# Routed rows scattered to token order, and two shared-expert tiles placed between the last two down products

## The chip, the cores and the metric

The kernel runs on 1 core of one Trainium2 chip. The metric is device time in microseconds for one execution; the median of 3 runs before the change is 1626.27 us (1625.15 to 1630.43). The profile is of one further execution.

## The reference

One layer over 1250 tokens of width 768, in float32: a graph network and a linear attention added to the tokens, and then a mixture-of-experts feed-forward, which is the part that matters here.

```
x = x + gnn(layernorm(x)) + linear_attention(layernorm(x))
xn = layernorm(x)
probs = softmax(xn @ router_w)                  # 8 experts
gates, idx = top_k(probs, 2); gates /= sum(gates)
routed = sum over the 2 picks: gate * ((silu(xn @ w_gate[e]) * (xn @ w_up[e])) @ w_down[e])
shared = (silu(xn @ ws_gate) * (xn @ ws_up)) @ ws_down      # hidden width 384
alpha  = sigmoid(xn @ sg_w + sg_b)
out = x + alpha * shared + (1 - alpha) * routed
```

Each expert has three 768x768 matrices (2304 KB each).

## The kernel before, in words

Tokens are kept as 10 tiles of 125 (`TP`, `NT`). `acc` holds the running sum of the layer on chip. After the graph and attention parts, each tile is normalised, written to DRAM as `xd` (by row) and transposed into `xnT`.

**Routing.** Each token has two picks, r = 0 and 1: 2500 rows of work. They are sorted by expert into parts of 64 rows (`PART`); two parts make a block of 128 rows. There are at most 26 blocks (`NBLK`), of which 22 (`NSURE`) always run; the others stand in nested `tc.If`s on the count of parts. `slot[:, r, t]` is the place of a row in that order. The DRAM table `who` takes, for each slot, the number of its token: 20 scatters on POOL's DMA queue (L898). It is then read back as `ids` (L904), on SP's queue.

**Shared expert.** While the tables are made, PE computes the shared expert's hidden rows into `hTs_s` (L942); its down product is left for the end of the kernel.

**Blocks.** For each block, `gather` fetches 128 rows of `xd` by index (POOL's queue, L973). `fetch(j, 0)`, `(j, 1)`, `(j, 2)` load the block's gate, up and down matrices into two-buffer rings `wg`, `wu`, `wd` (SP's queue, L985; the expert's number is read by a register load, L983). `rows` transposes the gathered rows, `gate` and `up` make the hidden rows, `hidden` transposes those, `down` makes the block's output. `product` (L1002) takes each half of the block from one of the two buffers of a ring, so that a block can straddle two experts; a fetch for the next block therefore waits for the present block's product with the same ring. The loop is software-pipelined by hand: in round j stand gate(j), hidden(j-1), up(j), rows(j+1), down(j-1). After each `down`, DVE copies the result out of PSUM (L1032) and ACT's queue writes the 128 rows to `ys` (L1033), block by block. `rings`' third member `wd` is allocated where `xnT` and the shared expert's weights lay; the other two are allocated earlier. Fetches are issued for one block beyond the 22.

**Join.** After the nested `tc.If`s (L1067) each engine meets the untaken path, on which its semaphores are stepped as the blocks would have done; before that, an engine that owns a DMA queue waits for its own transfers in flight.

**Combination.** For each token tile two gathers (POOL's queue, L1089) fetch the two rows of each token from `ys` by `slot`; PE makes the shared down product (12 matmuls of 125x384, L1097), and DVE adds `alpha` times it (L1100) and the two gated rows (L1102) to `acc`. Then the tile is stored, 120 rows by SP's queue and 5 by ACT's (L1105, L1106). `g2` holds the gates times 1 - `alpha`, `al` holds `alpha`.

The order on each engine is made by a tile framework from the program order and from the buffers: a scheduler can move an instruction ahead of others that it doesn't depend on, and waits are semaphores on engines and DMA lanes.

Of the kernel before, what the change touches and what calls it, by code (L numbers as in the profile page):

```python
# [8 lines left out]
F32 = mybir.dt.float32  # L9
# [53 lines left out]
def gps_block(ctx: ExitStack, tc: tile.TileContext, x, src, dst, norm_g, norm_b, W1, a_src1, a_dst1, b1,  # L63
# [7 lines left out]

    xd = dram.tile([N, D], F32, name="xd")
    who = dram.tile([NSLOT, 1], I32, name="who")
    ys = dram.tile([NSLOT, D], F32, name="ys")
    xd_t = xd.rearrange("(t p) d -> t p d", p=TP)
    who_b = who.rearrange("(b p) o -> b (p o)", p=P)
    who_p = who.rearrange("(b p) o -> p (b o)", p=P)
    ys_b = ys.rearrange("(b p) d -> b p d", p=P)
# [243 lines left out]
    with tc.tile_pool(name="cnt", bufs=1, reuse_waits="tile") as cp, \  # L322
# [3 lines left out]
        zero = cp.tile([P, D], F32, name="zero")  # L326
        nc.gpsimd.memset(zero, 0.0)
        nc.sync.dma_start(who_b, zero[:NBLK, :P].bitcast(I32))
        for j in range(NSURE, NBLK):
            nc.sync.dma_start(ys_b[j], zero)  # L330
# [282 lines left out]
    with tc.tile_pool(name="h2p", bufs=1, reuse_waits="tile") as hp, tc.tile_pool(name="gatw", bufs=2, reuse_waits="tile") as pw:  # L613
# [29 lines left out]
        ids = fp.tile([P, NBLK], I32, name="ids")  # L643
# [168 lines left out]
    with tc.tile_pool(name="fln", bufs=2, reuse_waits="tile") as pw, tc.tile_pool(name="flnps", bufs=2, space=PSUM, reuse_waits="tile") as ps:  # L812
# [17 lines left out]
        number = pw.tile([TP, NT], I32, name="number", bufs=1)  # L830
        nc.gpsimd.iota(number, pattern=[[TP, NT]], base=0, channel_multiplier=1)
# [64 lines left out]
        for t in range(NT):  # L896
            for r in range(2):
                put = nc.gpsimd.indirect_dma_start(  # L898
                    out=who, out_offset=bass.IndirectOffsetOnAxis(ap=slot[:, r, t:t + 1], axis=0),
                    in_=number[:, t:t + 1], in_offset=None, bounds_check=NSLOT - 1, oob_is_err=False)  # L900
                for p in puts:
                    tc.declare_no_dep(put.ins, p.ins, reason="slots differ")
                puts.append(put)
# [50 lines left out]
    with tc.tile_pool(name="fps", bufs=1, space=PSUM, reuse_waits="tile") as ps:  # L954
# [16 lines left out]
        def gather(j):  # L971
            if j < NBLK:
                nc.gpsimd.indirect_dma_start(  # L973
                    out=xin[j % 2], out_offset=None, in_=xd,
                    in_offset=bass.IndirectOffsetOnAxis(ap=ids[:, j:j + 1], axis=0),
                    bounds_check=N - 1, oob_is_err=False)

        def fetch(j, i):

            if j >= NBLK:  # L980
                return
            if i == 0:
                experts[j] = nc.sync.value_load(blk[0:1, j:j + 1], min_val=0, max_val=NE - 1)  # L983
            w = (w_gate, w_up, w_down)[i]
            nc.sync.dma_start(rings[i][:, j % 2], w[bass.ds(experts[j], 1)].rearrange("o (k p) f -> p (o k) f", p=P))  # L985
# [42 lines left out]
        def down(j):  # L1028
            y = yo[j % 2]
            for s in two:  # L1030
                product(j, 2, pd[:, s], hTs[j % 2], s)
            nc.vector.tensor_copy(y.rearrange("p (s d) -> p s d", s=2), pd[:, :, :HALF])  # L1032
            nc.scalar.dma_start(ys_b[j], y)  # L1033


        for j in two:
            gather(j)
            for i in range(2):
                fetch(j, i)
            if j == 0:  # L1040
                fetch(j, 2)
        places(0)
        rows(0)
        for j in range(NSURE):
            gate(j, 0)
# [3 lines left out]
            if j > 0 and j + 1 < NSURE + 1:  # L1049
                fetch(j + 1, 0)  # L1050
            if j + 1 < NSURE:
                places(j + 1)
            for s in two:
                up(j, s)
            if j > 0 and j + 1 < NSURE + 1:
                fetch(j + 1, 1)
            gather(j + 2) if j + 2 < NSURE + 1 else None
            if j + 1 < NSURE:
                rows(j + 1)
# [3 lines left out]
        hidden(NSURE - 1)  # L1063
        down(NSURE - 1)
        fetch(NSURE, 2)

        with ExitStack() as deeper:  # L1067
            for j in range(NSURE, NBLK):
                deeper.enter_context(tc.If(n_part > j * NPART))
                gather(j + 1)  # L1070
# [4 lines left out]
                fetch(j + 1, 0)  # L1075
                for s in two:
                    up(j, s)
                fetch(j + 1, 1)
                hidden(j)
                down(j)  # L1080
                fetch(j + 1, 2)
# [3 lines left out]
    with tc.tile_pool(name="comb", bufs=1, reuse_waits="tile") as cb, tc.tile_pool(name="cps", bufs=3, space=PSUM, reuse_waits="tile") as ps:  # L1085
        ygs = [cb.tile([TP, D], F32, name=f"yg{i}") for i in range(2 * NT)]
        for t in range(NT):
            for r in range(2):
                nc.gpsimd.indirect_dma_start(  # L1089
                    out=ygs[2 * t + r], out_offset=None, in_=ys,  # L1090
                    in_offset=bass.IndirectOffsetOnAxis(ap=slot[:, r, t:t + 1], axis=0),
                    bounds_check=NSLOT - 1, oob_is_err=False)
        for t in range(NT):
            pd = ps.tile([TP, 2, 512], F32, name="pds")
            for s in range(2):
                for f in range(nh):
                    nc.tensor.matmul(pd[:, s, :HALF], hTs_s[:, f, t * TP:(t + 1) * TP],  # L1097
                                     wsd[:, f, s * HALF:(s + 1) * HALF], start=(f == 0), stop=(f == nh - 1))
            av = acc[:, t, :].rearrange("p (s d) -> p s d", s=2)
            nc.vector.scalar_tensor_tensor(av, pd[:, :, :HALF], al[:, t:t + 1], av, op0=ALU.mult, op1=ALU.add)  # L1100
            for r in range(2):
                nc.vector.scalar_tensor_tensor(acc[:, t, :], ygs[2 * t + r], g2[:, t, r:r + 1], acc[:, t, :],  # L1102
                                               op0=ALU.mult, op1=ALU.add)

            nc.sync.dma_start(out_t[:TP - 5, t, :], acc[:TP - 5, t, :])  # L1105
            nc.scalar.dma_start(out_t[TP - 5:, t, :], acc[TP - 5:, t, :])  # L1106

# [26 lines left out]
```

## Time and profile before

| what | value |
|---|---|
| median of 3 runs | 1626.27 us (1625.15 to 1630.43) |
| the profiled execution: time, span | 1627.49 us, 1625.8 us |
| mean granted TensorE clock | 0.977 |
| busy PE, DVE, ACT, POOL | 94%, 44%, 23%, 9% of the span |
| a block in the steady run, on PE | 25.13 us |
| PE idle before the down product, waiting for `wd` | 9.2 us, once |
| POOL gathers of `yg` | 20, 1.33 us each |
| DVE sums of `yg` rows, 125x768 | 20, 1.02 us each |
| PE shared down product | 120 matmuls, 42.0 us |

The page divides the span into busy shares by engine, names the chain of work that ended last, and lists groups of equal instructions with the idle time before them and what ended it. A line such as "PE A <- DMA B: 9.2, 1, 9.2" means that PE's instructions A waited for the transfer B for 9.2 us in total, once, at most 9.2 us. PE, DVE, ACT and POOL are the compute engines, SP only issues transfers; a "q" after a name is the engine's sequencer, which also issues its DMAs.

### The profile page before, as it was taken

To read this page: it belongs to the slowest core of one execution; us is meant where nothing else is said; L and a number is where in the kernel's file an instruction comes from. 1 tells how busy PE (TensorE), PEld (TensorE's weight loads), DVE (VectorE), ACT (ScalarE), POOL (GpSimd) and SP (SyncE) were. 2 spreads that over 40 slices of the span, in tenths; PEclk is the share of its full clock that TensorE was granted. 3 is DMA by queue.
4 is the path that set the end of the run, shared out by engine and by line. 5 is a ranking of instruction groups with operands and counts; after the bars stand their busy time and mean duration, and the time that the engine had idled before them with its cause. 6 is when DMAs were issued, how large, how long until landed. Compare 5 with 4: busy or idle time off the path is not lost. (4 is left out here: it accounts for less than half of the span.)

```text
span 1625.8 us, 18650 instructions
## 1 busy us (share of the span) xinstructions
PE 1528.3 (94%) x7123; PEld 855.5 (53%) x7123; DVE 720.8 (44%) x1329; ACT 368.0 (23%) x630; POOL 140.4 (9%) x174
## 2 busy tenths in 40 slices
PE   6899889998999989999899998999999999999966
PEld 5566544444455678995455553444444444444433
DVE  7889639411625468996598531111111111111106
ACT  3222211111101058870367300101001111011000
POOL 2211000000000000000000142000000000000014
PEclk9999989999999999999999999999999999999988
DMA  8100042001201110002111366788888888888858
GB/s 237 39 1 1 2 128 66 4 0 38 72 20 49 30 45 32 32 17 75 32 60 48 106 92 159 293 310 315 325 315 310 306 314 314 316 319 311 308 171 262
DMA packets 104756, 238.83 MB, mean 147 GB/s; under 512 B 15735, under 2 KB 38391, under 8 KB 104663
## 3 DMA queue, kind: packets, MB, share of 16 engines
q1 hardware_dynamic: 84749, 192.43, 35.1%
q0 software_dynamic: 14544, 35.83, 7.4%
q10 hardware_dynamic: 5370, 9.30, 1.6%
q8 instruction: 63, 1.03, 0.3%
q14 instruction: 30, 0.25, 0.1%
HBM read 219.45 MB, written 18.02 MB: 146 GB/s over the span
## 5 line engine op out<-in xcount | busy, mean ns | idle before, releaser
L1002 PE MATMUL pdb<-wd,hT 128*64 128x384 f32 (+1 forms) x1056 | 176.9, 492 | 9.2 <-DMA wd<-in_L_ffn_w_down_dram 9.2
L1002 PE MATMUL pgb<-wg,xT 128*64 128x384 f32 (+1 forms) x1056 | 179.9, 491 | 0.2 <-ACT xT L1009 0.2
L1002 PE MATMUL pub<-wu,xT 128*64 128x384 f32 (+1 forms) x1056 | 174.0, 486 | 0.0
L539 PE MATMUL pp<-wkv,xnT 128*125 128x512 f32 x360 | 162.0, 599 | 0.1
L621 PE MATMUL pa<-G,u 125*125 125x199 f32 x800 | 140.4, 336 | 11.1 <-DVE h L629 6.0
L621 PEld LDWEIGHTS pa<-G,u 125*125 125x125 f32 x800 | 135.6, 189 | 16.2 <-issue 7.2
L1002 PEld LDWEIGHTS pdb<-wd,hT 128*64 128x64 f32 x1056 | 74.8, 138 | 100.7 <-issue 97.5
L1002 PEld LDWEIGHTS pub<-wu,xT 128*64 128x64 f32 x1056 | 75.6, 137 | 94.6 <-issue 94.6
L1002 PEld LDWEIGHTS pgb<-wg,xT 128*64 128x64 f32 x1056 | 74.0, 138 | 91.4 <-issue 90.6
L539 PEld LDWEIGHTS pp<-wkv,xnT 128*125 128x125 f32 x360 | 66.0, 190 | 74.0 <-issue 73.6
L1032 DVE COPY y<-pdb 128x768 f32<-128x768 f32 x22 | 21.1, 957 | 188.9 <-PE pdb L1002 188.9
L418 PE MATMUL ph<-wg,xnT 128*125 128x400 f32 x240 | 102.1, 532 | 2.7 <-PEq L432 2.6
L1021 DVE TENSOR_TENSOR h<-h,pgb 128x384 f32<-128x384 f32 x44 | 24.4, 554 | 181.0 <-ACT h L1020 181.0
L601 ACT ACTIVATE eb<-r,g_ss 125x625 f32<-125x625 f32 x120 | 95.0, 816 | 22.9 <-DVE ea L602 22.9
L602 DVE TENSOR_TENSOR ea<-ea,eb 125x625 f32<-125x625 f32 x120 | 94.0, 804 | 13.6 <-ACT eb L601 8.1
L604 DVE SCALAR_TENSOR_TENSOR u<-ea,cntT 125x625 f32<-125x625 f32 x120 | 94.0, 804 | 12.5 <-PE pa L621 8.0
L486 DVE CUSTOM_DVE_ANT_0 junk<-ssb,absent 125x1250 bf16<-125x1250 f32 x60 | 87.7, 1462 | 13.8 <-DMA ssb<-g_srow_d 12.5
L1020 ACT ACTIVATE h<-pgb 128x384 f32<-128x384 f32 x44 | 21.6, 490 | 308.2 <-PE pgb L1002 308.2
L569 PE MATMUL pq<-xnT,wq 128*128 128x500 f32 (+1 forms) x216 | 81.5, 521 | 4.5 <-DMA wq<-in_L_mix_w_qkv_dram 3.7
L721 PE MATMUL pu<-wu,xnT 128*125 128x384 f32 x240 | 82.5, 489 | 2.0 <-DVE acc L726 2.0
L1026 DVE TENSOR_TENSOR h<-h,pub 128x384 f32<-128x384 f32 x44 | 24.4, 554 | 134.4 <-PE pub L1002 134.4
L582 PE MATMUL pu<-wp,at 128*125 128x384 f32 x240 | 80.4, 488 | 1.1 <-DVE acc L585 1.1
(247 smaller groups left out, 1699.2 us busy)
## 6 DMA issues: line engine op xcount, KB each, us to landing
wg<-in_L_ffn_w_gate_dram SPq DMA_DIRECT2D x23, 2304.0 KB
wu<-in_L_ffn_w_up_dram SPq DMA_DIRECT2D x23, 2304.0 KB, 10.2
wd<-in_L_ffn_w_down_dram SPq DMA_DIRECT2D x23, 2304.0 KB
ys<-y ACTq DMA_DIRECT2D x22, 384.0 KB, 7.1
r<-g_rrow_d POOLq DMA_DIRECT2D x12, 610.4 KB, 8.3
wq<-in_L_mix_w_qkv_dram SPq DMA_DIRECT2D x18, 384.0 KB, 3.4
wkv<-in_L_mix_w_qkv_dram SPq DMA_DIRECT2D x6, 768.0 KB, 4.6
acc<-in_x_dram POOLq DMA_DIRECT2D x10, 375.0 KB, 10.8
```

Source lines behind the costliest of these rows:

```text
L418: nc.tensor.matmul(ph[:, :2 * CG], xnT[:, k, tok], wg[:, k, s * 2 * CG:(s + 1) * 2 * CG], start=(k == 0), stop=(k == KD - 1))
L486: nc.vector.tensor_tensor_reduce(out=junk, in0=self.ssb, in1=absent[:, dt, :], scale=1.0, scalar=-3.0e38, op0=ALU.add, op1=ALU.max, accum_ ...
L539: nc.tensor.matmul(pp, xnT[:, k, tok], wkv[:, k, :, :], start=(k == 0), stop=(k == KD - 1))
L569: nc.tensor.matmul(pq[:, :qw], wq[:, k, :], xnT[:, k, tok], start=(k == 0), stop=(k == KD - 1))
L582: nc.tensor.matmul(pu[:, s, :HALF], at[:, k, i * TP:(i + 1) * TP], wp[:, k, s * HALF:(s + 1) * HALF], start=(k == 0), stop=(k == KD - 1))
L601: nc.scalar.activation(eb, r[:, 1, :], AF.Exp, bias=ss02[:, st, h:h + 1])
L602: nc.vector.tensor_max(ea, ea, eb)
L604: nc.vector.scalar_tensor_tensor(u, ea, 1.0, cntT[:, st, half * W:(half + 1) * W], op0=ALU.min, op1=ALU.mult)
L621: nc.tensor.matmul(pa[i][:, :CO + 1], u[:, i * TP:(i + 1) * TP], G[:, st, h, :CO + 1], start=(st == 0), stop=(st == NT - 1))
L721: nc.tensor.matmul(pu[:, :HALF], xnT[:, k, t * TP:(t + 1) * TP], wus[s][:, k, :], start=(k == 0), stop=(k == KD - 1))
L1002: nc.tensor.matmul(pt[part, :HALF], rows[:, k, part], w[:, k, s * HALF:(s + 1) * HALF], start=(k == 0), stop=(k == KD - 1))
L1021: nc.vector.tensor_mul(h, h, pgs[s][:, :HALF])
```

## The change

- `who` has two columns: the token (where a row is read) and the token plus r times 1250 (where its result goes). `number` holds both, for r = 0 and 1. Slots with no row get 0 and 2500.
- `ys` is no longer in slot order but in token order: 1250 rows for r = 0, 1250 for r = 1, and three rows at the end that are set to zero. `down` writes by an indirect scatter on POOL's queue, by `ids[:, j, 1]`; an index of 2500 is out of bounds and writes nothing. The zero writes of the blocks that may not run are gone.
- The combination loads both rows of a token tile with one ordinary load on SP's queue, 128 rows of which 125 are used: 10 loads instead of 20 gathers.
- The shared down product is a function, in two halves of 384. Two of its ten tiles stand between `hidden(NSURE - 1)` and `down(NSURE - 1)`, in the PSUM banks of the gate and up products; the other eight stay in the combination. There the sums of `yg` rows start after the fourth tile, two token tiles a step, and stores follow when both parts are in.
- Fetches and gathers are no longer issued for block 23 of the loop (j = 22); a block in a `tc.If` fetches its own. At the start `fetch(0, 2)` comes after the fetches of blocks 0 and 1.

```diff
-    who = dram.tile([NSLOT, 1], I32, name="who")
-    ys = dram.tile([NSLOT, D], F32, name="ys")
+    who = dram.tile([NSLOT, 2], I32, name="who")
+    ys = dram.tile([2 * N + P - TP, D], F32, name="ys")
...
-        zero = cp.tile([P, D], F32, name="zero")
-        nc.gpsimd.memset(zero, 0.0)
-        nc.sync.dma_start(who_b, zero[:NBLK, :P].bitcast(I32))
-        for j in range(NSURE, NBLK):
-            nc.sync.dma_start(ys_b[j], zero)
+        nobody = cp.tile([NBLK, P, 2], I32, name="nobody")
+        nc.gpsimd.iota(nobody, pattern=[[0, P], [2 * N, 2]], base=0, channel_multiplier=0)
+        nc.sync.dma_start(who_b, nobody.rearrange("b p o -> b (p o)"))
+        rest = cp.tile([P - TP, D], F32, name="rest")
+        nc.gpsimd.memset(rest, 0.0)
+        nc.sync.dma_start(ys[2 * N:, :], rest)
...
-        number = pw.tile([TP, NT], I32, name="number", bufs=1)
-        nc.gpsimd.iota(number, pattern=[[TP, NT]], base=0, channel_multiplier=1)
+        number = pw.tile([TP, 2, NT, 2], I32, name="number", bufs=1)
+        for r in range(2):
+            nc.gpsimd.iota(number[:, r], pattern=[[TP, NT], [r * N, 2]], base=0, channel_multiplier=1)
...
-            nc.scalar.dma_start(ys_b[j], y)
+            nc.gpsimd.indirect_dma_start(
+                out=ys, out_offset=bass.IndirectOffsetOnAxis(ap=ids[:, j, 1:2], axis=0),
+                in_=y, in_offset=None, bounds_check=2 * N - 1, oob_is_err=False)
+
+        def shared(t, banks):
+            for s, pt in enumerate(banks):
+                half = slice(s * HALF, (s + 1) * HALF)
+                for f in range(nh):
+                    nc.tensor.matmul(pt[:TP, :HALF], hTs_s[:, f, t * TP:(t + 1) * TP], wsd[:, f, half],
+                                     start=(f == 0), stop=(f == nh - 1))
+                nc.vector.scalar_tensor_tensor(acc[:, t, half], pt[:TP, :HALF], al[:, t:t + 1], acc[:, t, half],
+                                               op0=ALU.mult, op1=ALU.add)
...
         for j in two:
             gather(j)
             for i in range(2):
                 fetch(j, i)
-            if j == 0:
-                fetch(j, 2)
+        fetch(0, 2)
...
         for j in range(NSURE):
+            more = j + 1 < NSURE
...
-            if j > 0 and j + 1 < NSURE + 1:
+            if j > 0 and more:
                 fetch(j + 1, 0)
...
-            gather(j + 2) if j + 2 < NSURE + 1 else None
+            if j + 2 < NSURE:
+                gather(j + 2)
...
         hidden(NSURE - 1)
+
+        shared(0, pgs)
+        shared(1, pus)
         down(NSURE - 1)
-        fetch(NSURE, 2)
...
-        ygs = [cb.tile([TP, D], F32, name=f"yg{i}") for i in range(2 * NT)]
+        ygs = [cb.tile([P, 2, D], F32, name=f"yg{t}") for t in range(NT)]
         for t in range(NT):
-            for r in range(2):
-                nc.gpsimd.indirect_dma_start(
-                    out=ygs[2 * t + r], out_offset=None, in_=ys,
-                    in_offset=bass.IndirectOffsetOnAxis(ap=slot[:, r, t:t + 1], axis=0),
-                    bounds_check=NSLOT - 1, oob_is_err=False)
-        for t in range(NT):
-            pd = ps.tile([TP, 2, 512], F32, name="pds")
...
+            nc.sync.dma_start(ygs[t], bass.AP(tensor=ys.tensor, offset=ys.offset + t * TP * D,
+                                              ap=[[D, P], [N * D, 2], [1, D]]))
+
+        def store(t):
             nc.sync.dma_start(out_t[:TP - 5, t, :], acc[:TP - 5, t, :])
             nc.scalar.dma_start(out_t[TP - 5:, t, :], acc[TP - 5:, t, :])
+
+        done = []
+        for t in range(2, NT):
+            pd = ps.tile([TP, 2, 512], F32, name="pds")
+            shared(t, [pd[:, s, :] for s in range(2)])
+            if t == NT - 1:
+                store(t)
+            if t < 3:
+                continue
+            for u in range(2 * (t - 3), min(2 * (t - 3) + 2, NT)):
+                for r in range(2):
+                    nc.vector.scalar_tensor_tensor(acc[:, u, :], ygs[u][:TP, r, :], g2[:, u, r:r + 1], acc[:, u, :],
+                                                   op0=ALU.mult, op1=ALU.add)
+                if u < NT - 1:
+                    done.append(u)
+            while done and done[0] <= t:
+                store(done.pop(0))
```

## The prediction

> **What bounds the kernel now.** I read three stretches: where the expert blocks begin, their steady run, and the tail. The page names the tail as the chain that ended last, so it comes first.
>
> ```profile
> span 1625.8 us, 18650 instructions
> ...
> DMA 1%; issue 1%; POOL 0%; DVE 0%; POOLq 0%; DVEq 0%
> ```
>
> The chain's first piece stands at 1576.37 us: the 20 gathers of `yg` on POOL, their transfers, the sums on DVE. The timeline dates the end: last DVE sum over at 1621.81, span over at 1625.8, so 4.0 us for the last store. The waits of that stretch:
>
> ```profile
> POOL yg L1089 <- SPq L1067: 87.4, 1, 87.4
> ...
> PE pdb L1002 <- DMA wd<-in_L_ffn_w_down_dram: 9.2, 1, 9.2
> ...
> PE pds L1097 <- DVE acc L1100: 4.4, 1, 4.4
> ...
> PE pds L1097 <- ACTq L1067: 2.3, 1, 2.3
> ```
>
> PE stands 9.2 us before the last block's down product: `fetch(21, 2)` is issued as down(20) ends, and the next work is the product that needs it. SP's own waits hold a 9.2 us piece at L1067, the join of the untaken branch, where it waits for the weight load it had just issued for a block that never runs. The tail in time:
>
> ```profile
> 1555.97 9.79 PE L1002 MATMUL pdb<-wd,hT 128*64 x48 [9.22 <-DMA wd<-in_L_ffn_w_down_dram]
> ...
> 1565.77 0.37 SPq L985 DMA_DIRECT2D wd<-in_L_ffn_w_down_dram  x1
> 1565.82 0.96 DVE L1032 COPY y<-pdb 128x768 f32<-128x768 f32 x1 [18.85 <-PE pdb L1002]
> 1566.81 0.33 ACTq L1033 DMA_DIRECT2D ys<-y  x1
> ...
> 1577.39 1.28 POOL L1089 DMA_INDIRECT yg<-ys,slot  x1 [87.37 <-SPq L1067]
> ```
>
> From the copy's end (1566.78) to the first gather 10.6 us pass. The last of the 20 gathers is issued at 1608.58, 31.2 us after the first, 1.64 us apart, and the DMA engines are full beside them (stretches: busy columns PE, PEld, DVE, ACT, POOL, then PE clock, DMA share, GB/s):
>
> ```profile
> 1550.00:1558.00 8.00, 2.03 (x8) 0.95 (x10) 0.00 (x0) 0.00 (x0) 0.00 (x0) 0.50 0.62 240
> ...
> 1600.00:1605.00 5.00, 5.00 (x17) 2.88 (x16) 2.92 (x4) 0.00 (x0) 4.09 (x4) 1.00 1.00 313
> ...
> 1010.00:1015.00 5.00, 5.00 (x34) 2.23 (x32) 1.11 (x2) 0.49 (x1) 0.00 (x0) 1.00 1.03 413
> ...
> 1085.00:1110.00 25.00, 25.00 (x158) 11.39 (x156) 3.17 (x5) 2.70 (x6) 1.00 (x1) 1.00 0.87 314
> ```
>
> The last line is the steady run: PE busy all 25 us of a 25.13 us block, DMA at 0.87. PE bounds it. At its start PE waits for the first gather:
>
> ```profile
> 990.33 0.37 SPq L904 DMA_DIRECT2D ids<-who  x1
> ...
> 995.54 1.07 POOL L973 DMA_INDIRECT xin<-xd,ids  x1 [11.28 <-DMA ids<-who]
> ...
> 999.64 1.51 PE L1008 MATMUL ptr<-ident,xin 128*128 128x128 f32 x6 [7.68 <-DMA xin<-xd,ids]
> ```
>
> **The change part by part.** Times are of the profiled execution.
>
> *Setup.* A 26x256 iota and a 3-row memset stand for the 0.74 us memset on POOL; SP loses four 384 KB zero writes (33.2 to 36.9 us). SP's next load waits until 52.85 and the DMA engines stand at 0.00 in 40 to 50 us, so 0. If that cover were gone: 1.57 MB at the 389 GB/s of that stretch (245 at share 0.63), 4 us, a gain. The second iota of `number` (20 values a row; POOL idles 23.5 us before the `who` scatters) costs 0. The scatters and `ids` carry 8 bytes where they carried 4, with as many pieces: 0, bounded by plus 1 us.
>
> *Start of the blocks.* In the built order SP issues `fetch(0,2)` after the loads for block 1. Before, wd(0) stood behind 21 register loads of `blk` (0.61 us each, 12.8 us: 990.7 to 1003.4), and wg(1), wu(1) behind it. Now those two, 4.7 MB, go right behind `ids`, at about 991.4, and take until about 1005 at 413 GB/s. `gather(0)` at 995.5 falls among them. Alone it landed in 4.0 us; at share 1.03 the gather of 1018.96 took 6.2, and the median of all is 7.0. PE waits for it alone, so plus 2.2 to 3.0; I take **+2.8**, near the median (`ids` ahead of them may also end later: bound plus 5; a gain is excluded, as nothing before the gather got shorter). wd(0) leaves at about 1004, as before, and nothing waited for wg(1).
>
> *Steady run.* Each block's 384 KB leave by POOL's queue, not ACT's. Bytes are the same; rows of empty slots are out of bounds (22 x 128 - 2500 = 316 rows fewer). POOL has 1.00 us of 25 busy; the issue adds about 1. The scatter waits for DVE's `y` copy, and behind it stands the gather two blocks ahead: that moves from about 1061.8 to 1071.5, needed at 1110.9, cover 39 us against 8.6 us of landing at worst. Its scatter waits also for the one before, 25 us older. Here the skill speaks against the change: the DMA: Bandwidth & Descriptors page, "Issuing engine by pattern", gives plain loads and stores to the sync and scalar queues and calls that path generally faster. The rows: `ys` from ACT landed in a median 7.1 us, gathers from POOL in 7.0; alone, the 360 KB store took 3.0 and the gather 4.0. By the rule one would charge 1 us a block, 22 in sum, if anyone waited; `y` has two buffers, 25 us of cover, so only the last block's is exposed. I take **0** (bounds -0.5 and +2).
>
> *Last block.* 24 matmuls of two shared tiles now stand between hidden(21), over at 1546.7, and down(21). 48 such matmuls took 15.75 us, so 7.9, to 1554.6: inside the wait, which ends at 1555.9 as before. wu(22), now gone, landed 8.1 us after 1538.23, before wd(21) started, so I give no gain for it; at best wd lands 1.3 us earlier. DVE's four 125x384 sums (about 0.55 us each) end before the `y` copy. What is gained is the clock: 0.50 after the wait, so down(21) took 9.79 us against 7.96 elsewhere. It ends at 1563.85 instead of 1565.76: **-1.9** (bounds -3.2 and -0.5).
>
> *Join.* Copy over at 1564.9. Scatter from POOL, landing 4.3 us alone (nearest row, the two gathers at 996): 1569.2. POOL's join waits for all its transfers, then steps their semaphores (that one instruction took 1.08 us at 1489), which SP's first load waits for: 1570.4. First gather before: 1577.39. Of these 7.0 us, 1.9 are counted: **-5.1** (bounds -6.5 and -1; several such steps or a slow receipt would eat it). SP's 9.2 us wait goes with its load. PE's 2.3 us wait for ACT goes too, off the path.
>
> *Tail.* Twenty gathers become ten SP loads of 786 KB (128 rows, two runs of 3 KB). First landing: a 360 KB store alone took 3.0, so about 2.1 fixed, plus 786 KB at 370 GB/s (314 at share 0.86), 2.1, plus issue 0.4: 4.6 us, at 1575.0. Later ones every 2.1 us. DVE takes longer: two sums of 1.02 a tile and sixteen half sums of 0.55; after that landing 20 x 1.02 + 15 x 0.55 = 28.7 us, so **DVE becomes the bound**, ending at 1603.7. PE needs 96 x 0.328 = 31.5 us from 1564.6 and has three PSUM buffers: its fourth tile waits for DVE from 1576.4 to about 1578.8, then follows DVE. The skill's TensorE: Matmul & The Clock Gate page, "What's actually happening", puts the drop to half clock after about 3.4 us of idling; here a 4.4 us wait was followed by 0.62 and 0.63. At 2.4 us the rule says full clock, sum unchanged. If it dropped for one such window PE would lose 1.7 us, shared with DVE's slack: 0 to +1.5. Loads end at about 1594; 3.8 MB of stores follow behind them in SP's queue, about 11 us at 350 GB/s, so they drain with DVE. From first transfer's issue to last sum: 33.3 us instead of 44.4, **-11.1**. Last store 4.0 us, as before.
>
> Sum: +2.8 - 1.9 - 5.1 - 11.1 = **-15.3**; span 1610.5, with the 1.7 us around it (1627.49 against 1625.8) 1612.2. The profiled execution lies 1.2 above the median of 1626.27, so the median becomes **1611.0**.
>
> **The rivals.**
>
> *The tail is DMA-bound at its old rate.* 11.7 MB at 290 to 313 GB/s, seen with share 1.0, is 39 us: 1571 + 39 + 2 = 1612, not 1607.7, so 5 us worse: 1616. For it: reads and stores mix, and the stores use 120 rows. Against: those rates held gathers through POOL's queue, which the page's table puts at 298 GB/s of engine time (35.83 MB in 7.4% of the span), the loads' queue at 337.
>
> *Cheap start, quick join.* xin lands in 5, down(21) starts early: 1607.
>
> *Slower: the weights come late.* Each fetch has 17 us (wd issued at 1069.43, needed at 1086.5) and lands in 8 to 10.3. Scatter and gather now come back to back, just as wd is fetched: 0.39 MB more, 1.3 us. From a landing of 17.1 us each microsecond costs 21; at 18.2, 25 us, and 1636; the sign turns at 17.7. That is 6 us more than I see (10.3 + 1.3).
>
> *The tiles don't lie in the wait.* PE's built order puts them there; excluded.
>
> **How the numbers follow.** Main case 0.62 (1607 to 1615), DMA-bound tail 0.20 (1613 to 1620), cheap start 0.10 (1604 to 1608), a DMA-bound tail with start and join near their bad bounds (+2.2 and +4.1 more: 1622) 0.04, late weights 0.04. The range 1604.5 to 1619 leaves out the last two and the outer ends. 0.3% is 4.9 us, about what a measurement of this kernel tells from no change. Faster 0.93, same 0.03, slower 0.04.
>
> **What would show it.** PE's 9.2 us wait for wd gone or under 2 us; down(21) near 8 us; first `yg` load near 1573 (1570 plus the start's 2.8); DVE nearly solid from there, 29 us; PE's wait for the first xin 10 to 11 us; PE solid in the blocks with a period of 25.1. It is wrong if DVE waits for `yg` over 5 us in sum after the first, if PE waits for weights inside the blocks, or if the first load leaves after 1577.

## The result, and the profile after

| | median | runs | ratio to the kernel before, 95% interval |
|---|---|---|---|
| before | 1628.33 us | 1625.15 to 1630.43 | |
| after | 1605.24 us | 1604.45 to 1606.43 | 0.986 (0.9839 to 0.9882) |

The 1628.33 us are the median of four runs of the kernel before: the three named at the head and one more, taken beside the kernel after. The change is faster by 1.4%, some 23 us. The prediction said 1611.0 and a range from 1604.5 to 1619.0, so the time lies in the range, at its fast end. The profiled execution has a span of 1603.0 us, 22.8 us less than before (1625.8).

I cut both spans at the same seven events and compare stage by stage. The timeline dates each event: by the start of a line, and for the copy of `y` and the last sum by the end of the line (start plus duration).

| stage | before | after | difference | predicted |
|---|---|---|---|---|
| A: start to the first scatter of `who` | 947.3 | 945.3 | -2.0 | 0 |
| B: to the first transpose of block 0 (PE) | 52.3 | 44.5 | -7.8 | +2.8 |
| C: to the fetch of `wd` for block 21 | 546.3 | 544.9 | -1.5 | 0 |
| D: to the end of the last `y` copy | 20.8 | 19.0 | -1.8 | -1.9 |
| E: to the first transfer of `yg` | 10.6 | 5.0 | -5.6 | -5.1 |
| F: to the end of the last sum on DVE | 44.4 | 40.3 | -4.1 | -11.1 |
| G: to the end | 4.0 | 4.1 | +0.1 | 0 |
| sum | 1625.8 | 1603.0 | -22.8 | -15.3 |

So the total is near the forecast, but two terms are far off in opposite directions: the start of the blocks (B and C) gave 9.3 us where a loss of 2.8 was expected, and the tail (F) gave 4.1 where 11.1 were expected.

The page of the kernel after, its span and the engines' shares of the chain:

```profile
span 1603.0 us, 18665 instructions
...
issue 32%; PE 30%; DVE 11%; DMA 8%; POOL 4%; ACT 3%; POOLq 0%; SPq 0%; DVEq 0%; ACTq 0%
```

"issue" has 32% here and had 1% before. In the blocks this chain now runs along POOL's queue, from a scatter of `ys` to the next gather and back, with long "issue" pieces between, while PE works through (25.00 of 25 us, below). It is the chain that was released last, but not what bounds the kernel; stages and waits have to be read instead. The waits from 1500 us on (total, times, longest):

```profile
DVE acc L1045 <- PE pds L1043: 9.6, 6, 3.4
...
PE pds L1043 <- DVE acc L1045: 9.1, 2, 6.7
...
DVE acc L1122 <- DMA yg<-ys: 7.1, 1, 7.1
...
PE pdb L1003 <- SPq L1083: 1.5, 1, 1.5
```

The same stretch of the kernel before had, besides the waits that the prediction shows:

```profile
DVE acc L1102 <- DMA yg<-ys,slot: 19.3, 10, 10.8
...
DVE acc L1100 <- PE pds L1097: 5.5, 1, 5.5
```

In the list of the kernel after, the last line answers to the 9.2 us wait for `wd`: 1.5 us are left (the profile names SP's queue as the releaser; the product starts 10.0 us after its weights were issued). The third is DVE's wait for the first `yg`; after it, DVE waits for no load, where before it waited ten times. But PE and DVE now wait about twice as long for each other: PE 9.1 us for DVE (4.4 before), and DVE 9.6 us for PE (5.5 before). The timeline from the last blocks on (start, duration, engine, line, instructions in a group):

```profile
1534.66 0.37 SPq L986 DMA_DIRECT2D wd<-in_L_ffn_w_down_dram  x1
...
1535.28 4.03 PE L1043 MATMUL pgb<-wsd,hTs_s 128*125 128x384 f32 x12
...
1544.69 7.96 PE L1003 MATMUL pdb<-wd,hT 128*64 x48 [1.51 <-SPq L1083]
1552.69 0.96 DVE L1033 COPY y<-pdb 128x768 f32<-128x768 f32 x1 [8.86 <-PE pdb L1003]
1553.62 7.33 PE L1043 MATMUL pds<-wsd,hTs_s 128*125 128x384 f32 x22 [0.97 <-PEq L1083]
...
1558.62 2.98 SPq L1103 DMA_DIRECT2D yg<-ys  x5
...
1563.54 3.00 DVE L1122 SCALAR_TENSOR_TENSOR acc<-yg,g,acc 125x768 f32<-125x768 f32 x3 [7.09 <-DMA yg<-ys]
...
1567.64 2.92 PE L1043 MATMUL pds<-wsd,hTs_s 128*125 128x384 f32 x4 [6.69 <-DVE acc L1045]
```

The down product takes 7.96 us, the first load leaves 5.0 us after the copy's end (1553.65), and the first sum starts 4.9 us later, all as forecast. Then PE stops at 1560.95 (1553.62 + 7.33) for 6.69 us, before it has made the second of its eight tiles. (A tile is 6 matmuls, three for each half, and the trace holds two records of each: 12 records a tile, of which 22 have run. The table of the kernel before and the prediction count these records as matmuls; their times are not touched by that.) The stretches (PE, PEld, DVE, ACT, POOL, then PE clock, DMA share, GB/s):

```profile
1085.00:1110.00 25.00, 25.00 (x158) 11.41 (x156) 3.18 (x5) 2.70 (x6) 1.92 (x3) 1.00 0.86 313
1560.00:1565.00 5.00, 0.95 (x3) 0.20 (x2) 1.43 (x2) 0.00 (x0) 0.00 (x0) 1.00 0.95 348
1565.00:1570.00 5.00, 2.35 (x4) 1.43 (x5) 4.96 (x7) 0.00 (x0) 0.00 (x0) 0.51 1.04 409
1570.00:1575.00 5.00, 5.00 (x13) 2.73 (x13) 3.44 (x5) 0.00 (x0) 0.00 (x0) 0.80 1.03 394
```

The first line is the steady run, unchanged but for POOL's 1.92 us. In the tail the loads run at 394 to 409 GB/s, faster than the gathers did (290 to 313); PE comes back at a clock of 0.51, and in 1570 to 1575 DVE has 3.44 us of work and PE is what it waits for.

### The profile page after: what moved, and what is told of

Same layout as the page of the kernel before. It is cut to its first block, busy times and chain, and to the rows that moved or that the text cites. A ratio compares the mean times of both kernels' runs of the same rounds, so it can differ in the third digit from the quotient of the medians.

```text
span 1603.0 us, 18665 instructions
## 1 busy us (share of the span) xinstructions
PE 1524.3 (95%) x7123; PEld 854.2 (53%) x7123; DVE 721.8 (45%) x1339; ACT 367.9 (23%) x630; POOL 136.6 (9%) x177
## 4 chain that ended last, share of the span: by engine, by line
issue 32%; PE 30%; DVE 11%; DMA 8%; POOL 4%; ACT 3%; POOLq 0%; SPq 0%; DVEq 0%; ACTq 0%
PE pp L542 6%; PE pu L585 5%; PE pq L572 5%; DVE junk L489 4%; DMA ys<-y,ids 4%; PE pa L624 4%; DVE ea L605 2%; PE pn L740 2%; PE pn L577 2%; ACT eb L604 2%; ACT ea L602 1%; POOL xin L976 1%; DVE u L607 1%; PE pds L1043 1%; POOL ys L1034 1%
## 5 line engine op out<-in xcount | busy, mean ns | idle before, releaser
L624 PE MATMUL pa<-G,u 125*125 125x199 f32 x800 | 140.4, 336 | 11.1 <-DVE h L632 6.0
L489 DVE CUSTOM_DVE_ANT_0 junk<-ssb,absent 125x1250 bf16<-125x1250 f32 x60 | 87.8, 1463 | 13.7 <-DMA ssb<-g_srow_d 12.4
```

The costliest lines, as they stand in the source:

```text
L489: nc.vector.tensor_tensor_reduce(out=junk, in0=self.ssb, in1=absent[:, dt, :], scale=1.0, scalar=-3.0e38, op0=ALU.add, op1=ALU.max, accum_ ...
L624: nc.tensor.matmul(pa[i][:, :CO + 1], u[:, i * TP:(i + 1) * TP], G[:, st, h, :CO + 1], start=(st == 0), stop=(st == NT - 1))
```

## Experiments

Each compares with the kernel before, run beside it. A difference in us is the ratio's distance from 1, times 1629 us. The stage letters are those of the table above.

| kernel | median us | ratio (95%) | A | B | C | D | E | F |
|---|---|---|---|---|---|---|---|---|
| before | | | 947.3 | 52.3 | 546.3 | 20.8 | 10.6 | 44.4 |
| after | 1605.24 | 0.986 (0.9839 to 0.9882) | 945.3 | 44.5 | 544.9 | 19.0 | 5.0 | 40.3 |
| b_who8 | 1616.71 | 0.9918 (0.9903 to 0.9933) | 947.1 | 44.5 | 544.8 | 20.9 | 11.0 | 43.8 |
| b_who4s | 1616.91 | 0.9917 (0.9901 to 0.9934) | 945.2 | 44.4 | 544.9 | 20.7 | 10.9 | 45.4 |
| b_who64 | 1617.95 | 0.9933 (0.9918 to 0.9948) | 945.3 | 44.4 | 544.9 | 20.9 | 11.5 | 43.6 |
| b_nopre | 1621.77 | 0.9954 (0.9938 to 0.997) | 945.5 | 53.3 | 547.2 | 20.2 | 5.0 | 43.7 |
| b_tiles | 1627.48 | 0.9987 (0.9977 to 0.9997) | 945.8 | 53.4 | 546.6 | 19.0 | 11.3 | 43.4 |
| a_fetch | 1604.66 | 0.9858 (0.9836 to 0.9879) | 945.5 | 44.5 | 544.9 | 18.9 | 5.0 | 40.5 |
| a_bufs4 | 1607.28 | 0.9865 (0.9847 to 0.9884) | 948.4 | 44.5 | 544.9 | 18.9 | 5.6 | 39.7 |
| a_notiles | 1606.64 | 0.987 (0.9849 to 0.9891) | 944.5 | 44.6 | 544.9 | 20.8 | 5.6 | 40.0 |
| a_split | 1597.17 | 0.9803 (0.9788 to 0.9818) | 945.9 | 44.5 | 544.8 | 18.9 | 5.0 | 32.1 |
| s_notiles | 1603.55 | 0.9847 (0.9829 to 0.9865) | 954.6 | 44.5 | 544.9 | 21.0 | 5.8 | 36.7 |
| s_gather | 1612.49 | 0.9897 (0.9884 to 0.9911) | 947.3 | 45.9 | 544.9 | 19.0 | 6.9 | 45.5 |
| a_whole4o | 1595.05 | 0.979 (0.9778 to 0.9803) | 946.9 | 44.9 | 544.9 | 19.0 | 5.3 | 29.7 |

Stage A varies from 944.5 to 954.6 us between profiled executions, and kernels whose code up to there is that of before (b_nopre, b_tiles) have 945.5 and 945.8. The 2.0 us of stage A are therefore no effect of the change that these runs can show. The other stages scatter less, and not all alike. Where the code is the same, B has 52.3 to 53.4 with the old `who` and 44.4 to 44.6 with most of the new ones; D repeats to 0.2; E has 10.6 to 11.5 with the old join and 5.0 to 5.8 with the new one (6.9 in s_gather), and F has 43.6 to 45.4 with the tail of before. The readings below rest on differences larger than these.

### Why the blocks start earlier: the table `who`

b_who8 is the kernel before with `who` two columns wide:

```diff
-    who = dram.tile([NSLOT, 1], I32, name="who")
+    who = dram.tile([NSLOT, 2], I32, name="who")
...
-                    in_=number[:, t:t + 1], in_offset=None, bounds_check=NSLOT - 1, oob_is_err=False)
+                    in_=number[:, t, :], in_offset=None, bounds_check=NSLOT - 1, oob_is_err=False)
```

> The kernel before with one edit: each row of who has two columns, so the 20 scatters and the ids load carry 8 bytes a row where they carried 4; the second column is not used. Theory (the start was gained by quicker scatters): their landing falls from a median 12.4 us to about 8.4, POOL's 8.1 us of waits for them goes, ids leaves about 11 to 12 us earlier, PE's 7.7 us wait for the first xin goes, with 1.5 us of half clock behind it: 8 to 9 us faster than before. Rival (the start was gained by the order of the first weight loads, and the scatters fell with something else that the change moved): scatters stay at 12 us, time as before within 1 us.

b_who4s writes 4 bytes a row as before, into rows 8 bytes apart; b_who64 does the same with rows 64 bytes apart (16 in place of 2):

```diff
+        slot2 = pw.tile([TP, 2, NT], I32, name="slot2", bufs=1)
+        nc.vector.tensor_scalar(slot2, at, 2.0, None, op0=ALU.mult)
...
-                    out=who, out_offset=bass.IndirectOffsetOnAxis(ap=slot[:, r, t:t + 1], axis=0),
+                    out=who, out_offset=bass.IndirectOffsetOnAxis(ap=slot2[:, r, t:t + 1], axis=0),
```

> The kernel before with 4-byte scatters, but into rows that lie 8 bytes apart (the slot is doubled for the address, one more DVE instruction of 20 values a row). It parts the size of a row from its spacing. If the size counts: scatters land as before (median 12.4 us), time as before within 1 us. If what counts is that 4-byte rows lie side by side in one 8-byte unit: landing about 8.4 us and 8 to 9 us faster than before, like the 8-byte rows.

> The kernel before with 4-byte scatters into rows that lie 64 bytes apart. With rows 8 bytes apart, whether 4 or 8 bytes were written, ids left 3.5 us after the last scatter's start and the time fell by 13 us. If what costs is two rows in one 8-byte unit: the same again, ids 3.5 us after the last scatter, DMA share about 0.65 in 945 to 985 us. If rows that share a longer stretch (64 bytes) hold each other up as well: DMA share under 0.5 there and ids up to 2 us earlier. Either way the time is within 2 us of the kernel with rows 8 bytes apart, because the shared expert's hidden product covers the first gather by then.

All three give the whole of the change's gain at the start: B falls from 52.3 to 44.4 or 44.5, C to 544.8 or 544.9. b_who8 and b_who4s are 13 us faster by their ratios (11 to 16), where 8 to 9 were expected; b_who64 is 11. The two stages account for 9.3 to 9.4 us. Of the rest, some 3 us lie in which executions were profiled: that of the kernel before took 1627.49 us, 2 less than its median here (1629.5), that of b_who8 1617.81, 1 more than its own. So the rival (the order of the first loads) falls, and the width written doesn't matter either: 4 bytes spaced out do what 8 bytes do. What counts is how densely the rows lie. The waits for the scatters, and the time from issue to landing (min/median/max), in the kernel before:

```profile
  POOL who L898: 8.1, 3
...
DMA to landing us min/median/max: 5.4/12.4/18.9
```

in the kernel after, and then in b_who64:

```profile
DMA to landing us min/median/max: 3.7/8.4/10.4
```

```profile
DMA to landing us min/median/max: 2.5/3.9/7.5
```

With rows side by side a scatter takes 12.4 us (13.1 and 13.6 in b_nopre and b_tiles), with rows 8 bytes apart 8.4 (up to 9.3 in the other kernels with the changed `who`), with rows 64 bytes apart 3.9. The traces of b_who8 and b_who4s hold no landing times; there POOL's waits for the scatters show the gain, 0.3 us and none in place of 8.1. The share of the DMA engines in 945 to 985 us goes the same way: 0.87 before, 0.64 in b_who8, 0.66 in b_who4s, 0.48 in b_who64, with nearly the same number of packets in all (104756 in the first three, 104862 in the last). In the kernel after POOL issues one scatter each 1.5 us; in the kernel before, at 12 us and more, it had to wait for earlier ones, 8.1 us in all, and the last landed late too (7.2 us from its issue to the load of `ids`, against 3.9). The first hypothesis of b_who64 (only an 8-byte unit counts) is out: spacing beyond 8 bytes shortens the landing further, though the kernel gains nothing more by it, since PE no longer waits for the gather. Why close rows cost more is not shown here. The Trainium skill's DMA: Bandwidth & Descriptors page, "Specifications", says that transfers below 512 B are done as read-modify-write; rows that share the stretch read and written back could then hold each other up. That fits, but no run here shows it.

With POOL's waits gone, the gather of block 0 is issued at 982.26 instead of 995.54, while PE is still on the shared expert's hidden rows, and PE's 7.68 us wait for it vanishes:

```profile
984.78 5.19 PE L946 MATMUL pu<-xnT,wsu 128*128 128x500 f32 x12
989.81 0.82 PE L1009 MATMUL ptr<-ident,xin 128*128 128x128 f32 x6
```

After the wait of before, PE's clock was 0.67 in 1000 to 1005 us; that accounts for the 1.5 us of stage C, which is longer (by 1.5 to 2.4 us) in each kernel with the wait and in none without it.

a_fetch is the kernel after with the old order of the first loads:

```diff
         for j in two:
             gather(j)
             for i in range(2):
                 fetch(j, i)
-        fetch(0, 2)
+            if j == 0:
+                fetch(j, 2)
```

> The changed kernel with the old order of the first loads: wd(0) ahead of the gather and the two loads of block 1. Theory (the first gather lands well before the shared expert's hidden product frees PE, now that ids is early): the gather lands in about 4 to 5 us and not 7.2, nobody waits for either, time within 1 us of the changed kernel. Rival (the order of the first loads is what sped up the start): PE waits 3 us or more for xin or wd again, 3 to 8 us slower.

The chain of waits of the kernel after (start, duration):

```profile
973.91 3.66 DMA who<-number,slot
...
977.78 3.63 DMA ids<-who
...
982.26 7.19 DMA xin<-xd,ids
```

and of a_fetch:

```profile
982.66 4.00 DMA xin<-xd,ids
```

The prediction's collision is real: among the loads for block 1 the gather lands 3.2 us later (7.19 against 4.00). But it lands at 989.45, and PE's shared product ends at about 989.8, so nobody waits; the two times agree (0.9858 and 0.986). It just fits: in s_gather, below, where POOL waited 9.6 us for `ids` to land and not 7.2, PE waited 0.62 us for the gather, and in a_whole4o 0.31.

### The join: a weight load that nobody uses

b_nopre is the kernel before without the loads issued ahead for block 22:

```diff
-            if j > 0 and j + 1 < NSURE + 1:
+            if j > 0 and j + 1 < NSURE:
...
-        fetch(NSURE, 2)
```

> The kernel before without the gather and the three weight loads issued ahead for block 22, which never runs; the untaken block would issue its own. Theory (SP's join waited for the weight load just issued for that block): SP's 9.2 us wait at the join goes, the first gather leaves 5 to 6 us after the last copy's end and not 10.6: 4 to 5.5 us faster. Rival (the join was long for another reason, the store of ys through ACT or the steps of the semaphores): first gather still 9 to 10.6 us after the copy, time within 1 us of before.

```profile
1565.21 0.96 DVE L1032 COPY y<-pdb 128x768 f32<-128x768 f32 x1 [18.22 <-PE pdb L1002]
...
1571.15 1.28 POOL L1087 DMA_INDIRECT yg<-ys,slot  x1 [106.24 <-SPq L1066]
```

From the copy's end (1566.17) to the first gather 4.98 us pass, where it was 10.6; the kernel after has 4.97. That is all of stage E's gain, and the store's way (ACT's queue here, POOL's there) makes no difference to it. By its ratio the kernel is 7.5 us faster (5 to 10), where 4 to 5.5 were expected; E gives 5.6 of them, and the rest is not assigned. SP had issued a load of 2304 KB for a block that never runs and waited for it at the join.

### The two tiles between the last down products

b_tiles adds them to the kernel before, a_notiles takes them out of the kernel after:

```diff
         hidden(NSURE - 1)
-
-        shared(0, pgs)
-        shared(1, pus)
         down(NSURE - 1)
...
-        for t in range(2, NT):
+        for t in range(NT):
```

> The kernel before with the two tiles of the shared down product between the last two blocks' down products, as in the change, and eight left in the tail, each summed over 768 columns at once. Theory (the tail hangs on the 20 gathers, so two tiles less of PE and DVE there are worth little): PE's wait for wd falls from 9.2 to about 1.5 us, down(21) takes 8.0 instead of 9.8, the first gather is about 2 us earlier, the last sum too: 2 to 3 us faster. Rival (the tail was bounded by PE or DVE): 8 us faster, the time of two tiles on PE.

> The changed kernel with all ten shared tiles in the tail, as before, and none between the last two down products. Theory (with plain loads the tail hangs on PE and DVE, so here the two tiles count, which in the kernel before were worth 2 us): PE's wait for wd is 9 us again, down(21) takes 9.3 to 9.8 us, the first yg load is 1.5 us later, and the two tiles cost 4 to 8 us more in the tail: 5 to 9 us slower than the changed kernel. Rival (the tail hangs on the loads): 1.5 to 2.5 us slower.

In b_tiles:

```profile
1555.83 7.96 PE L1002 MATMUL pdb<-wd,hT 128*64 x48 [1.54 <-DMA wd<-in_L_ffn_w_down_dram]
...
1576.11 1.28 POOL L1102 DMA_INDIRECT yg<-ys,slot  x1 [86.30 <-PE pds L1111]
```

and SP's own waits:

```profile
SPq L1080 <- SPq L1080: 10.4, 2, 9.9
```

Stage D falls by 1.8 us, as in the change, through the clock alone: 7.96 us for the down product instead of 9.79. Counted from the fetch of `wd`, the first gather leaves 1.1 us earlier, not 2, as SP still waits 9.9 us for the unused load at the join. The whole is worth 2 us (0.5 to 3.7), at the lower end of what was expected. F is 43.4, against 43.6 to 45.4 with ten tiles: with gathers, two tiles less in the tail show no clear gain there.

a_notiles missed: 5 to 9 us slower were expected, and it is slower than the kernel after by 1.6 us, with intervals that overlap. D is 1.8 longer, and F is no longer at all (40.0 against 40.3) with two tiles more to do. Its waits say where they went:

```profile
PE pds L1043 <- DVE acc L1045: 2.7, 1, 2.7
```

PE's 9.1 us of waits in the tail have become 2.7. In the changed kernel the two tiles were taken out of a stretch in which PE then stood. What they brought there is thus the 1.8 us of the clock in D, and no gain in F.

### Why the tail gained only 4 us

In the built order (the profile leaves buffer numbers out), PE does the first half of tile 2, two matmuls of tile 3, the second half of tile 2, the rest of tile 3's first half and two matmuls of tile 4: 11 matmuls, the 22 records above. Next comes the second half of tile 3. It goes to the same two-bank PSUM tile as the first half, and waits until DVE has read the first half. DVE has that read sixth in its tail:

```
sum of tile 2, first half
yg 0, row 0     <- waits for the first landing
yg 0, row 1
yg 1, row 0     <- needs the second load
sum of tile 2, second half
sum of tile 3, first half
```

So PE waits, through DVE, for the first loads and three sums of their rows: these start at 1563.54, the two sums behind them end at 1567.59, and PE goes on at 1567.64. Two theories were left: this wait inside a tile, or the three PSUM buffers that the prediction had named.

```diff
-            pd = ps.tile([TP, 2, 512], F32, name="pds")
-            shared(t, [pd[:, s, :] for s in range(2)])
+            shared(t, [ps.tile([TP, 512], F32, name=f"pds{s}") for s in range(2)])
```

> The changed kernel with one edit: in the tail each 384-wide half of a shared tile has its own one-bank PSUM tile (three buffers each, six banks as before) in place of one two-bank tile for both. Theory (a tile's second half waits until DVE has read its first half, and DVE has sums of yg ahead of that read that wait for the first landing): PE runs through tiles 2, 3 and 4 while DVE waits, PE's waits for DVE fall from 9.1 us to under 3, its clock holds, DVE is nearly solid after the first landing: last sum 33 to 36 us after the first load's issue in place of 40.3, so 4 to 8 us faster than the changed kernel (about 1597 to 1601). Rival (three buffers, or DVE's order alone, limit PE): within 1 us of the changed kernel's 1605.

```diff
-    with ... tc.tile_pool(name="cps", bufs=3, space=PSUM, reuse_waits="tile") as ps:
+    with ... tc.tile_pool(name="cps", bufs=4, space=PSUM, reuse_waits="tile") as ps:
```

> The changed kernel with four two-bank PSUM buffers for the tail's shared tiles in place of three. It tests the limit that the prediction named (the fourth tile waits for a buffer). Theory of the halves: PE stops inside a tile, before a fourth buffer is ever asked for, so PE's waits stay at about 9 us and the time within 1 us of the changed kernel. Rival (buffers limit): PE's waits fall to under 4 us, 4 to 6 us faster.

With a fourth buffer the wait stays, and the time with it (0.9865):

```profile
PE pds L1043 <- DVE acc L1045: 9.0, 2, 6.6
```

With a PSUM tile for each half it is gone (a_split; timeline, then waits):

```profile
1554.30 31.20 PE L1043 MATMUL pds<-wsd,hTs_s 128*125 128x384 f32 x96 [1.17 <-PEq L1083]
```

```profile
DVE acc L1121 <- DMA yg<-ys: 6.8, 1, 6.8
DVE acc L1045 <- PE pds L1043: 2.4, 1, 2.4
```

PE makes all 96 records in one piece at full clock, and DVE, once the first load is in, is solid to the end at 1591.15. F is 32.05 us, against 40.3; the kernel takes 0.9803 of the time of before, 8 to 9 us less than the change. The scheduler still puts sums of `yg` ahead of the shared sums here (two of them stand before the second half of tile 2), so it is the wait inside the tile, not that order by itself, that cost 8 us.

With this wait gone, the other parts of the tail can be tried again. s_notiles is a_split with ten tiles in the tail; s_gather is a_split with 20 gathers from the token-ordered `ys` in place of the ten loads (`number`, their index, moves to a buffer that lasts so long):

```diff
-            nc.sync.dma_start(ygs[t], bass.AP(tensor=ys.tensor, offset=ys.offset + t * TP * D,
-                                              ap=[[D, P], [N * D, 2], [1, D]]))
+            for r in range(2):
+                nc.gpsimd.indirect_dma_start(
+                    out=ygs[t][:TP, r, :], out_offset=None, in_=ys,
+                    in_offset=bass.IndirectOffsetOnAxis(ap=number[:, r, t, 1:2], axis=0),
+                    bounds_check=2 * N - 1, oob_is_err=False)
```

> The kernel with separate PSUM tiles for the halves (1597 us), with all ten shared tiles in the tail and none between the last two down products. In the changed kernel itself leaving the two tiles in the tail cost only 1 to 2 us, since PE ran them while it would have stood. Theory (that stall hid them): here nothing stands, the start of the loads comes 1.8 us later (down(21) at half clock), and DVE has four more half sums, 2.2 us, of which the wait for the first landing hides some: 2.5 to 4.5 us slower than 1597. Rival (the two tiles are worth nothing anywhere): within 1 us of 1597.

```profile
1565.23 38.94 PE L1043 MATMUL pds<-wsd,hTs_s 128*125 128x384 f32 x120 [1.35 <-PEq L1080]
...
1605.20 2.19 DVE L1045 SCALAR_TENSOR_TENSOR acc<-pds,al,acc 125x384 f32<-125x384 f32 x4
```

```profile
DVE acc L1118 <- DMA yg<-ys: 8.2, 2, 5.8
DVE acc L1045 <- PE pds L1043: 3.9, 2, 2.5
```

Here the two tiles count: F is 36.7 instead of 32.1, and D and E 2.9 longer; by the ratios 7 us, more than the 2.5 to 4.5 expected. PE works without a stop to 1604.17, but it is not the bound: both of DVE's waits for PE lie before the first landing, and from 1590.25 to the end at 1607.39 DVE has no gap. Of the 4.6 us of F, three half sums more after the first landing are 1.7 us, and a second wait of DVE for a `yg` load is 2.4 us; why that load came late is not shown. The profiled execution is the slowest of its five (1613.45, median 1603.55), but the excess lies in stage A, 8.7 us longer than in a_split.

> The kernel with separate PSUM tiles for the halves (1597 us), but the ten loads of yg are again 20 gathers on POOL, of 125 rows each, here from the token-ordered ys. Theory (with PE free, what made the short tail possible is that the bytes come by ten loads issued in 15 us and not by 20 gathers issued 1.6 us apart): the last gather is issued 30 us after the first, DVE waits for yg again, first issue to last sum is 40 to 44 us and not 32: 8 to 12 us slower than 1597, so 1605 to 1609. Rival (the change of the loads was worth nothing, all came from the order of the shared tiles): within 2 us of 1597.

```profile
DVE acc L1124 <- DMA yg<-ys,number: 24.2, 9, 13.7
```

With gathers F is 45.5, no shorter than before (44.4), and DVE waits 24.2 us for rows in place of 6.8; PE in turn waits 10.8 us for DVE. The loads are thus worth 13.4 us of F once the halves have their own PSUM tiles, and without them neither the tiles nor the split shorten the tail. Whether it is the other queue or the smaller number of transfers is not parted here. The 15 us of the ratios are more than the 8 to 12 expected: the gathers also start 1.9 us later after the join, and stage B is 1.4 longer. No run takes the loads alone out of the change itself, so its 4.1 us of F are not divided.

### A faster version

a_whole4o takes the lesson back into the change: one 768-wide sum a tile, as in the kernel before, four buffers, and each `yg` sum kept behind the shared sum that precedes it in the text.

```diff
...
+            av = acc[:, t, :].rearrange("p (s d) -> p s d", s=2)
+            last = nc.vector.scalar_tensor_tensor(av, pd[:, :, :HALF], al[:, t:t + 1], av, op0=ALU.mult, op1=ALU.add)
...
+                    tc.add_manual_dep(add.ins, last.ins.name, mybir.DependencyInfo(
+                        mybir.DependencyClass.NoSync, mybir.DependencyReason.DATA), reason="order")
```

> The changed kernel with the tail's shared tiles summed over 768 columns at once from one two-bank PSUM tile, as in the kernel before, four such buffers, and DVE's order kept as written (a tile's sum ahead of the yg sums that follow it in the text). Theory (DVE is the bound of the tail once PE runs free): DVE does the sums of tiles 2 and 3 while it waits for the first landing and has 20 x 0.94 + 6 x 0.94 = 24.5 us after it, against 26.0 with the halves apart; last sum 30 to 31 us after the first load's issue: 1 to 2 us faster than 1597, so about 1595.5. Rival (the loads, 394 to 416 GB/s while they run, or the stores now bound the tail): within 0.5 us of 1597.

```profile
1570.00:1575.00 5.00, 5.00 (x17) 2.93 (x16) 5.00 (x7) 0.00 (x0) 0.00 (x0) 1.00 1.03 401
1575.00:1580.00 5.00, 5.00 (x17) 2.88 (x16) 5.00 (x6) 0.00 (x0) 0.00 (x0) 1.00 1.03 403
```

PE, DVE and the DMA engines are all full at once. F is 29.7 us, and the time 0.979 of before: the lowest median of these kernels, 34 us under before and 11 under the change. Against a_split it is 2.1 us by the medians, with overlapping intervals; in the profiled executions F is 2.3 us shorter and E 0.3 longer. The three edits were not tried one by one.

## Why the prediction was right, and where not

*Setup, 0.* Nothing in these runs contradicts it, and stage A scatters too much to confirm it.

*Start of the blocks, +2.8: wrong in sign; -9.3 was measured.* The size of the step that I priced was right: the gather among the loads lands 3.2 us later. The two sentences that failed are "The scatters and `ids` carry 8 bytes where they carried 4, with as many pieces: 0" and the exclusion of a gain because "nothing before the gather got shorter". The scatters did get shorter, from a median of 12.4 us to 8.4, POOL's 8.1 us of waits for them went, and the gather moved so far ahead that its 3.2 us were covered. The trace of before had those waits (POOL for `who`, 8.1 us in 3) a few lines from rows that I did quote. The range for this term should have allowed a gain. Two of the named signs failed with it: PE's wait of 10 to 11 us for the first xin was none at all, and the first `yg` load left at 1558.6, not near 1573.

*Steady run, 0: right.* C is 544.85 us in the kernel after and 544.84 in b_who8, which still stores `ys` from ACT's queue. The 22 scatters on POOL cost nothing, as nobody waited for them. The section "Issuing engine by pattern" of the Trainium skill's DMA: Bandwidth & Descriptors page, which the prediction weighed against the change, gives only plain transfers to the sync queue; the new store is an indirect one, for which the same table names GpSimd, so the rule did not speak against it.

*Last block, -1.9: right,* -1.8, and through the clock, as b_tiles shows alone.

*Join, -5.1: right,* -5.6. b_nopre shows that the dropped load is all of it, to within the scatter of this stage (5.0 to 5.8).

*Tail, -11.1: mis-sized; -4.1 was measured.* First landing (4.6 us forecast, 4.9 measured) and loads that outrun DVE were right. What failed is "has three PSUM buffers: its fourth tile waits for DVE from 1576.4 to about 1578.8". PE stopped in its second tile, for 6.69 us, as the halves share a PSUM tile. With that wait removed F is 32.05, near the forecast 33.3: the limit by DVE was the right mechanism of a tail without this stall. The point named as "DVE nearly solid from there" is where the profile shows the miss.

*The clock in the tail: wrong as well.* I took from the Trainium skill's TensorE: Matmul & The Clock Gate page, "What's actually happening", that a wait of 2.4 us stays under the 3.4 us of idling that bring half clock. PE's second wait in the tail was 2.43 us, and the clock fell:

```profile
1591.00:1592.00 1.00, 0.00 (x0) 0.00 (x0) 1.00 (x2) 0.00 (x0) 0.00 (x0) 1.00 0.15 43
...
1593.00:1594.00 1.00, 1.00 (x3) 0.44 (x2) 0.00 (x0) 0.00 (x0) 0.00 (x0) 0.50 0.38 151
1594.00:1595.00 1.00, 1.00 (x3) 0.56 (x2) 0.00 (x0) 0.00 (x0) 0.00 (x0) 0.50 0.00 0
...
1596.00:1597.00 1.00, 1.00 (x4) 0.59 (x4) 0.62 (x1) 0.00 (x0) 0.00 (x0) 1.00 0.00 0
```

Twelve records took 5.80 us there and take 4.03 at full clock: 1.8 us of the missing 7.0, at the very end of the path. In the trace of before, the clock after the 4.4 us wait was 0.50 from 1588 to 1592; the 0.62 that the prediction gives is a mean over 1590 to 1595. The same section calls the window in which the idling is counted free-running; read so, it could let a wait of 3.35 us pass (below), but not bring half clock after 2.43. What did is open.

*The rivals.* The DMA-bound tail didn't happen: the loads ran at 394 to 409 GB/s. "Cheap start" named a time close to the result (1607), though through a landing in 5 us, where it was 7.19 and covered. The weights never came late, and the tiles lay in the wait. The total came out near the forecast since two errors of 12.1 and 7.0 us cancel in part: that the time lies in the range is to this extent luck.

## What to carry to other kernels

Before costing a later transfer, look at what waits for the small transfers ahead of it: twenty scatters of single words held the start of the main loop, and spacing their rows apart was worth 9 of the 23 us. When a product's output is split into halves so that each can be summed early, and waits are kept for whole tiles as here, give each half its own PSUM tile, or the second half of the product waits for the reader of the first and for all that stands before that reader on its engine. A loop that prefetches one step beyond its end pays for it at the first point that waits for all transfers.

## What the runs showed of the hardware that I had not expected

- Indirect scatters of 125 rows of 4 bytes take longer the closer their rows lie in DRAM: a median of 12.4 to 13.6 us with rows side by side, 8.4 to 9.3 us with rows of 8 bytes at 8 bytes spacing, and 3.9 us with 4 bytes at 64 bytes spacing. Whether 4 or 8 bytes are written at a spacing of 8 made no difference to stage B (44.4 and 44.5 us).
- The clock does not follow the length of a wait alone: it fell to 0.50 after a wait of 2.43 us (and again in a_fetch and a_bufs4, after 2.43), and stayed at 1.00 in s_gather after one of 3.35 us, while one of 3.18 us there brought 0.50. A wait of 2.4 us is thus no assurance of full clock, while 1.5 us waits (before the last down product) left its 7.96 us untouched.
